# Where the product that sums the exponentials stands, and in which shape it runs, in a two-layer graph network kernel

## The chip, the cores and the metric

The kernel runs on one core of one Trainium2 chip. The metric is device time in microseconds of a whole execution, lower is better. A core has TensorE (PE, the matrix products; PEld are its weight loads), VectorE (DVE), ScalarE (ACT), GpSimd (POOL) and SyncE (SP, which here issues most of the transfers). Each engine works off its own queue of instructions in order, and waits on semaphores for others.

## The reference, cut to what matters

Sixteen graphs of 1024 nodes with 256 features go through an attention layer, whose queries come from a product with the weighted adjacency, and through a graph convolution with two batch norms. All is float32. The change lies in the softmax of the attention:

```
h  = relu(layernorm(x))                         # x: 16 x 1024 x 256
q  = relu((h^T @ (adj * A_s)) * para)           # 4 heads of 64
k, v = split(h @ kv_w)
attn = softmax(q @ k^T * scale, axis=-1)        # 1024 x 1024 for each head and graph
out  = attn @ v
x    = x + out
...                                             # layer 1: adjacency product, W1, batchnorm, W2, batchnorm
```

## The kernel before, in words

**Units and steps.** The attention works in units: one graph b, one chunk k of 128 features (two heads), and one half f of the queries (512 columns). There are 16 x 2 x 2 = 64 units. A unit takes four steps, each with two blocks of 128 keys. In a step, `scores` (line 882) makes the products sc of keys and queries, one for each head over 64 rows of the array, and ACT takes their exponentials p. One step later, `values` (line 922) multiplies them with v into o, one product for each head into 64 columns of the array. The scores are therefore laid out as keys by queries, and the softmax's denominators are sums over partitions and over key blocks.

**The denominators.** DVE adds the exponentials of all key blocks up in `acc` (`add`). When a unit has ended, `fold` (line 942) transposes `acc` in squares of 32 and adds along the rows, once for each head, into `part`: 128 partitions by 2 x 16 numbers. What is left is to add over groups of partitions. `sums` (line 953) does it with a product: the constant matrix `same` (line 82), 128 x 128, times `part`, 32 columns, into a PSUM tile of the pool `ps_t`. Three small DVE operations (lines 969, 974, 975) pick the right group and make the reciprocals `inv`. A step later, `finish` (line 980) turns the unit's output o with four transposes on PE (ot), into the same pool, which has one buffer, and `add_output` scales it by `inv` and adds it to x.

**Products in halves.** Nearly all other products of the first stage go through the helper `product` (line 167), which makes a product of 128 output rows as two matmuls of 64 columns of the array each. A float32 product appears in the trace as two records for each matmul.

**The order of the work.** The kernel's order is written by hand in `attention` (line 1008); nothing reorders it. In step s, PE gets in turn: the scores of step s; the actions filed under `at_top`; if the background has stopped at a mark `TOP`, its next piece, which is eight transposes htp of the next graph's features (`transposed`, line 385, called by `prepare` and `background`), copied out of PSUM by ACT; the values of step s - 1; and then pieces of the background (products pg, pk, pv, pa, py of the neighbouring graphs) until the step's share of their estimated time is used up. The actions of a unit whose values are issued in step s are filed by the tuple `one`: the two folds at the end of steps s and s + 1, the sums at the top of step s + 3, the output's transposes at the top of step s + 4. For the very last unit the four are at steps s, s, s + 1 and s + 1.

```
for action in at_top.pop(s, ()):
    action()
if top:
    done += advance(bg)
    top = False
if s in adds:
    adds.pop(s)()
```

Of the kernel before, what the change touches and what calls it, by code (L numbers as in the profile page):

```python
# [23 lines left out]
def gnn_two_layers_kernel(  # L24
# [12 lines left out]
    nc = tc.nc  # L37
# [37 lines left out]
    UNITS = B * CC * NH  # L75
# [20 lines left out]
    def layers(shifted):  # L96
# [35 lines left out]
        def advance(pieces):  # L132

            due = queue[:]
            queue.clear()
            cost = next(pieces, None)
            for action in due:
                action()
            return cost

        def run(*parts):
            for part in parts:
                while advance(part) is not None:
                    pass
            while queue:
                queue.pop(0)()
# [20 lines left out]
        def product(dst, left, right, start, stop):  # L167

            for e in range(2):
                r = slice(e * HW, (e + 1) * HW)  # L170
                nc.tensor.matmul(dst[r], left[:, r], right, start=start, stop=stop)  # L171
# [622 lines left out]
        def background(b):  # L794

            if b == 0:
                differences(1)
                for k in range(CC):
                    yield TOP
                    transposed(1, k)  # L800
                    yield 1.0
                w, products, norm = weighers[1], keys_values(1), Norm(2, True).all()
                yield from weave(
                    islice(products, 4), (0, double(islice(w, 8))), (0, islice(norm, 4))
                )
                yield from weave(
                    plain_queries(1), (0, norm), (0, w), (5, graph()), (7, degrees())
                )
                differences(2)
                yield from islice(products, 2)  # L810
                yield from prepare(2, products)
                return
            before = hidden(b - 1)
            gather = aggregate(b - 1)
            if b + 1 < B:
                w, products, norm = weighers[b + 1], keys_values(b + 1), normed(b - 1)
                yield from weave(islice(products, 4), (0, islice(w, 4)))
                if b == 1:
                    load_later()
                yield from weave(queries(b + 1), (0, double(w)), (9, islice(norm, 5)))  # L820
                yield next(gather)
                yield from weave(products, (0, norm))
            else:
                yield from weave(endings.pop(), (2, normed(b - 1)))
                yield next(gather)
            if b + 2 < B:
                yield from weave(gather, (3, summed(b + 2)))
                yield from prepare(b + 2, before)
            elif b + 2 == B:

                yield from gather
                endings.append(before)
            else:
                yield from gather
                yield from weave(before, (0, normed_last()))
# [46 lines left out]
        def scores(b, k, f, g):  # L882


            made = []
            for m in (2 * g, 2 * g + 1):
                sc = ps_sc.tile([P, 2, FB], F32, tag="sc", name=f"sc_{b}_{k}_{f}_{m}")
                for e in range(2):
                    r = slice(e * HD, (e + 1) * HD)
                    nc.tensor.matmul(  # L890
                        sc[:, e, :],
                        ks[b][k][r, m * P : (m + 1) * P],
                        qs[b][k][r, f * FB : (f + 1) * FB],
                        start=True,
                        stop=True,
                    )
                pr = p4.tile([P, 2, FB], F32, tag="p", name=f"p_{b}_{k}_{f}_{m}")
                nc.scalar.activation(pr, sc, AF.Exp)  # L898
                made.append(pr)
            return made  # L900

        class Unit:
# [50 lines left out]
            def sums(self):  # L953

                b, k, f = self.at
                J = FB // P
                if k == f == 0:
                    invs[b] = p2.tile([P, CC, NH, J, 2], F32, tag="inv", name=f"inv_{b}")
                self.inv = invs[b][:, k, f]
                pt = ps_t.tile([P, FB], F32, tag="t", name=f"sums_{self.name}")[:, : 2 * J * NS]  # L960
                nc.tensor.matmul(  # L961
                    pt,
                    same.rearrange("p a r -> p (a r)"),
                    self.part.rearrange("p e c -> p (e c)"),
                    start=True,
                    stop=True,
                )
                tmp = p1.tile([P, 2 * J, NS + 1], F32, tag="group", name=f"group_{self.name}")
                nc.vector.tensor_mul(
                    tmp[:, :, :NS],  # L970
                    pt.rearrange("p (c a) -> p c a", a=NS),
                    group.unsqueeze(1).to_broadcast([P, 2 * J, NS]),
                )
                nc.vector.tensor_reduce(tmp[:, :, NS], tmp[:, :, :NS], AX.X, ALU.add)
                nc.vector.reciprocal(
                    self.inv.rearrange("p j e -> p e j"),
                    tmp[:, :, NS].rearrange("p (e j) -> p e j", e=2),
                )
# [29 lines left out]
        def attention():  # L1008

            units = [Unit(b, k, f) for b in range(B) for k in range(CC) for f in range(NH)]  # L1010
            steps = [(u, g) for u in units for g in range(NG)]
            per_graph = CC * NH * NG
            before = None
            at_top, at_end, adds = {}, {}, {}
            bg, done, total, top = iter(()), 0.0, 0.0, False
            for s in range(len(steps) + 2):
                if s < len(steps):
                    unit, g = steps[s]
                    b = unit.at[0]
                    if s % per_graph == 0:  # L1020
                        run(bg)
                        top = False
                        bg, done = background(b), 0.0
                        total = (37.6 if b > 0 else 41.0) * (b + 1 < B) + 24.0 * (b > 0) + 6.0 * (b + 2 < B)
                        total += 13.7 * (0 < b < B - 2) + 27.4 * (b == B - 1) + 3.0 * (b == 0)

                        total -= 10.3 * (b == B - 1)
                    made = scores(*unit.at, g)
                    due = total * (s % per_graph + 1) / per_graph
                else:  # L1030
                    due += 5.1
                for action in at_top.pop(s, ()):
                    action()
                if top:
                    done += advance(bg)
                    top = False
                if s in adds:
                    adds.pop(s)()
                if s < len(steps):
                    for pr in made:  # L1040
                        unit.add(pr)
                if before is not None:
                    (last, g_last), prs = before
                    last.values(g_last, prs)
                    if g_last == NG - 1:

                        one = (0, 0, 1, 1) if last.index == UNITS - 1 else (0, 1, 3, 4)
                        for e in range(2):
                            at_end.setdefault(s + one[e], []).append(lambda u=last, e=e: u.fold(e))
                        at_top.setdefault(s + one[2], []).append(last.sums)  # L1050
                        at_top.setdefault(s + one[3], []).append(last.finish)
                        adds[s + one[3]] = last.add_output
                while done < due and not top:
                    cost = advance(bg)
                    if cost is None:
                        break
                    if cost == TOP:
                        top = True
                        break
                    done += cost  # L1060
                for action in at_end.pop(s, ()):
                    action()
                before = (steps[s], made) if s < len(steps) else None
            run(bg)
# [375 lines left out]
```

## Time and profile before

| what | value |
|---|---|
| time, median of 3 runs | 2608.92 us (2606.27 to 2610.16) |
| span of the profiled execution | 2604.3 us |
| granted TensorE clock, mean | 0.991 |
| score products (line 890) | 509.0 us busy, 2048 records |
| value products (line 931) | 495.9 us busy, 2048 records |
| sums (line 961) | 26.4 us busy, 128 records, mean 288 ns |
| weight loads of the sums (line 961) | 19.2 us busy, 128 records, mean 189 ns |
| output transposes ot (line 986) | 42.5 us busy, 256 records |
| feature transposes htp (line 396) | 36.5 us busy, 256 records |

The span runs from the first to the last instruction of the profiled execution; the runs' times hold a little more around it. Matmuls overlap, so a record's mean length is longer than its share of the busy time. A shape such as 128\*64 gives the rows and columns of the array that a matmul uses, and 128x32 behind it the data that streams through.

### The profile page before, as it was taken

The numbers are of one execution on the slowest core, as the hardware profiler recorded it, in microseconds if no ns is written. First come the engines' busy times: TensorE is split into PE (matmuls) and PEld (weight loads), VectorE is DVE, ScalarE is ACT, GpSimd is POOL, SyncE is SP. The second block draws the span as 40 slices with busy tenths as digits, with TensorE's granted clock in tenths as the row PEclk, the third lists the DMA queues.
The fourth block names the chain that finished last, engine by engine and source line by source line (L and its number), as shares of the span: only waits on it lengthen the run. The fifth ranks groups of instructions, "written<-read, shape, count | busy, mean of one in ns | idle before, by whom it ended". The sixth has DMA issues, their size and how long they took to land.

```text
span 2604.3 us, 31375 instructions
## 1 busy us (share of the span) xinstructions
PE 2525.9 (97%) x11627; PEld 931.8 (36%) x11627; DVE 1822.7 (70%) x2837; ACT 1460.7 (56%) x2034; POOL 391.3 (15%) x456
## 2 busy tenths in 40 slices
PE   7999999999999999999999999999999999999994
PEld 3333333333333333333333333333333333334443
DVE  4768686867767686868677676858686776657774
ACT  6774565647474746656464747465564634335543
POOL 1540001000101000010001010000100001036653
PEclk9999999999999999999999999999999999999997
DMA  3654224152524343241525243433315242355459
GB/s 138 229 171 173 93 99 154 54 189 73 182 83 152 111 148 101 102 150 55 183 71 182 86 156 107 147 100 114 137 62 180 66 166 105 109 196 221 170 198 367
DMA packets 130915, 363.46 MB, mean 140 GB/s; under 512 B 15288, under 2 KB 32192, under 8 KB 124608
## 3 DMA queue, kind: packets, MB, share of 16 engines
q1 hardware_dynamic: 110144, 282.70, 31.3%
q0 software_dynamic: 20608, 78.66, 7.9%
q8 instruction: 94, 1.54, 0.2%
q14 instruction: 69, 0.57, 0.1%
HBM read 286.79 MB, written 74.51 MB: 139 GB/s over the span
## 4 chain that ended last, share of the span: by engine, by line
PE 87%; ACT 7%; DMA 2%; issue 2%; DVE 1%; SPq 0%; POOL 0%; POOLq 0%; DVEq 0%; ACTq 0%
PE sc L890 17%; PE o L931 16%; PE pa L171 15%; PE pg L171 14%; PE py L171 8%; PE m_f L1235 7%; PE pk L171 4%; PE pv L171 4%; ACT w L458 3%; DMA out_dram<-xo_f 2%; ACT p L898 2%; PE ot L986 1%; ACT w L466 1%; PE sums L961 1%; ACT ht L399 1%
## 5 line engine op out<-in xcount | busy, mean ns | idle before, releaser
L898 ACT ACTIVATE p<-sc 128x1024 f32<-128x1024 f32 x512 | 495.0, 1020 | 452.5 <-PE sc L890 452.1
L920 DVE TENSOR_TENSOR acc<-acc,p 128x1024 f32<-128x1024 f32 x384 | 472.2, 1230 | 143.2 <-ACT p L898 121.8
L890 PE MATMUL sc<-q,k 64*128 64x512 f32 x2048 | 509.0, 615 | 4.7 <-ACT p L898 4.6
L931 PE MATMUL o<-p,v 128*64 128x512 f32 x2048 | 495.9, 605 | 0.0
L171 PE MATMUL pg<-w,h_a 128*64 128x512 f32 x1600 | 357.9, 592 | 3.1 <-DVE q L612 2.3
L171 PE MATMUL pa<-aht,h_b 128*64 128x512 f32 x1536 | 344.0, 592 | 3.5 <-ACT h_b L341 3.4
L890 PEld LDWEIGHTS sc<-q,k 64*128 64x128 f32 x2048 | 175.9, 186 | 325.5 <-issue 284.4
L458 ACT ACTIVATE w<-cbc,csum 128x512 f32<-128x512 f32 x256 | 285.5, 1168 | 0.0
L171 PE MATMUL py<-at,w 128*64 128x512 f32 x1024 | 232.8, 597 | 8.4 <-ACT ht L399 7.0
L445 DVE SCALAR_TENSOR_TENSOR w<-w,adj 128x1024 f32<-128x1024 f32 x128 | 157.5, 1230 | 114.8 <-ACT w L466 110.8
L931 PEld LDWEIGHTS o<-p,v 128*64 128x64 f32 x2048 | 124.1, 136 | 250.3 <-issue 247.2
L171 PEld LDWEIGHTS pg<-w,h_a 128*64 128x64 f32 x1600 | 114.7, 137 | 232.0 <-issue 214.4
L746 POOL DMA_DIRECT2D y_d<-y x128 | 70.5, 551 | 795.0 <-ACT y L745 787.2
L171 PEld LDWEIGHTS pa<-aht,h_b 128*64 128x64 f32 x1536 | 110.8, 137 | 216.9 <-issue 208.3
L745 ACT ACTIVATE y<-py,vec 128x512 f32<-128x512 f32 x128 | 87.6, 684 | 142.3 <-PE py L171 119.7
L749 DVE BATCH_NORM_STATS2 stats<-y 128x6 f32<-128x512 f32 x128 | 85.7, 687 | 79.6 <-ACT y L745 79.5
L466 ACT ACTIVATE w<-w 128x1024 f32<-128x1024 f32 x128 | 135.2, 1056 | 1.7
L520 DVE TENSOR_TENSOR w<-w,w 128x1024 f32<-128x1024 f32 x112 | 132.8, 1217 | 1.5
L341 ACT ACTIVATE h_b<-x,lnsm_b 128x256 f32<-128x256 f32 x128 | 70.4, 609 | 110.7 <-DVE lnsm_b L330 110.7
L93 POOL TENSOR_SCALAR lnsm_b<-mv_b 128x4 f32<-128x4 f32 x32 | 12.1, 379 | 791.5 <-DVE mv_b L319 791.4
L171 PEld LDWEIGHTS py<-at,w 128*64 128x64 f32 x1024 | 72.2, 137 | 162.4 <-issue 129.8
L171 PE MATMUL pk<-ht,kvw_f 128*64 128x512 f32 x512 | 117.0, 599 | 1.5 <-ACT ht L399 1.5
(158 smaller groups left out, 2779.7 us busy)
## 6 DMA issues: line engine op xcount, KB each, us to landing
aht<-aht_d SPq DMA_DIRECT2D x224, 512.0 KB, 6.3
adj<-in_adj_dram SPq DMA_DIRECT2D x128, 512.0 KB, 4.4
y_d<-y POOLq DMA_DIRECT2D x128, 256.0 KB, 2.6
yin_f<-y_d SPq DMA_DIRECT2D x32, 1024.0 KB, 6.3
x<-in_x_dram SPq DMA_DIRECT2D x32, 512.0 KB, 5.1
para<-in_para_dram SPq DMA_DIRECT2D x64, 256.0 KB, 3.9
x_d<-x POOLq DMA_DIRECT2D x16, 1024.0 KB, 10.3
xo_f<-x_d SPq DMA_DIRECT2D x32, 512.0 KB, 8.6
```

The costliest lines, as they stand in the source:

```text
L171: nc.tensor.matmul(dst[r], left[:, r], right, start=start, stop=stop)
L445: nc.vector.scalar_tensor_tensor(w, w, 1.0, a, op0=ALU.add, op1=ALU.mult)
L458: nc.scalar.activation(w[:, t, :].rearrange("p (t q) -> p t q", q=P), cbc[:, q * NT // NH : (q + 1) * NT // NH], AF.Abs, bias=csum[:, th * ...
L466: nc.scalar.activation(made[i], made[i], AF.Tanh, scale=-0.5 / C)
L520: nc.vector.tensor_sub(block(i)[part], block(x)[part], block(y)[part])
L745: nc.scalar.activation(y, made, AF.Identity, bias=b1[:, j : j + 1])
L749: nc.vector.bn_stats(stats1[:, j, i, :], y)
L890: nc.tensor.matmul(sc[:, e, :], ks[b][k][r, m * P : (m + 1) * P], qs[b][k][r, f * FB : (f + 1) * FB], start=True, stop=True,)
L898: nc.scalar.activation(pr, sc, AF.Exp)
L920: nc.vector.tensor_add(self.acc, self.acc, pr)
L931: nc.tensor.matmul(self.o[r, :], vs[b][k][:, m, r], pr[:, e, :], start=(m == 0), stop=(m == NT - 1),)
L1235: nc.tensor.matmul(made, left[:, j, :], right[:, j, :], start=(j == 0), stop=(j == JH - 1))
```

## The change

The product in `sums` goes through `product`: two matmuls of 64 columns each in place of one of 128, on the same operands and into the same PSUM tile. And the sums of all units but the last are filed in a new list, `at_mid`, which is worked off behind the piece of the background that `TOP` announces, and ahead of the addition of outputs, of the accumulation and of the values. In steps without such a piece the order of the instructions stays as it was. The sums of the last unit stay in `at_top`, and go through `product` as well.

```
@@ sums
-                nc.tensor.matmul(
+                product(
                     pt,
                     same.rearrange("p a r -> p (a r)"),
                     self.part.rearrange("p e c -> p (e c)"),
-                    start=True,
-                    stop=True,
+                    True,
+                    True,
                 )
@@ attention
-            at_top, at_end, adds = {}, {}, {}
+            at_top, at_mid, at_end, adds = {}, {}, {}, {}
...
                 if top:
                     done += advance(bg)
                     top = False
+                for action in at_mid.pop(s, ()):
+                    action()
                 if s in adds:
                     adds.pop(s)()
...
-                        at_top.setdefault(s + one[2], []).append(last.sums)
+                        (at_top if last.index == UNITS - 1 else at_mid).setdefault(
+                            s + one[2], []
+                        ).append(last.sums)
```

## The prediction

> **What bounds the kernel now.** I read the page's first part, then the chain that ended last, then the groups of TensorE (PE), then the timeline around the changed product.
>
> The page's busy times and its chain by engine and line:
>
> ```profile
> PE 2525.9 (97%) x11627; PEld 931.8 (36%) x11627; DVE 1822.7 (70%) x2837; ACT 1460.7 (56%) x2034; POOL 391.3 (15%) x456
> ...
> PE 87%; ACT 7%; DMA 2%; issue 2%; DVE 1%; SPq 0%; POOL 0%; POOLq 0%; DVEq 0%; ACTq 0%
> PE sc L890 17%; PE o L931 16%; PE pa L171 15%; PE pg L171 14%; PE py L171 8%; PE m_f L1235 7%; PE pk L171 4%; PE pv L171 4%; ACT w L458 3%; DMA out_dram<-xo_f 2%; ACT p L898 2%; PE ot L986 1%; ACT w L466 1%; PE sums L961 1%; ACT ht L399 1%
> ```
>
> PE is on 87% of the chain, and the sums have 1% of it. VectorE (DVE) and ScalarE (ACT) have room on average. So time taken from PE counts, except where another engine is ahead of it for a stretch.
>
> Now a step without sums, the PE timeline at 508 us and its weight loads (PEld); columns are start, length, instruction, count:
>
> ```profile
> 507.75 0.60 PE L890 MATMUL sc<-q,k 64*128 64x512 f32 x2
> 508.27 0.65 PE L931 MATMUL o<-p,v 128*64 128x512 f32 x2
> ...
> 508.27 0.20 PEld L931 LDWEIGHTS o<-p,v 128*64 128x64 f32 x4 [0.76 <-issue]
> ```
>
> and one with sums, at 526 us:
>
> ```profile
> 525.65 0.59 PE L890 MATMUL sc<-q,k 64*128 64x512 f32 x2
> 526.17 0.41 PE L961 MATMUL sums<-part,same 128*128 128x32 f32 x2
> 526.51 0.65 PE L931 MATMUL o<-p,v 128*64 128x512 f32 x2
> ...
> 526.17 0.30 PEld L961 LDWEIGHTS sums<-part,same 128*128 128x128 f32 x2 [0.76 <-issue]
> ```
>
> From the last score pair to the first value pair it is 0.52 us without sums and 0.86 us with them: the sums insert 0.34 us, though they stream only 32 columns, twice (each fp32 product appears as two records). The third field of the shape shows why: scores are 64*128, sums 128*128, values 128*64, three array shapes in a row.
>
> **The 0.34 us taken apart.** In a run of values, pairs start every 0.427 us for 512 columns (0.83 ns per column). So after a score pair starts, its streaming ends 0.43 us later, and the next shape's first weight load comes at 0.52: 0.09 us of drain at a change of shape. A 128-column load takes 0.11 us (two sums loads, mean 189 ns, span 0.30, so the second starts 0.11 after the first). A 64-column load takes about 0.055: the four of the values, mean 136, span 0.20, and record by record they come as two pairs, 0.055 apart, the halves of a pair 6 ns apart. So with full-width sums: load 0.108, load 0.110, stream 32 x 0.83 = 0.027, drain 0.093. Together 0.338, as measured.
>
> A step in which the background's transposes (htp) come after the sums, at 455 us:
>
> ```profile
> 455.02 0.41 PE L961 MATMUL sums<-part,same 128*128 128x32 f32 x2
> 455.26 1.07 PE L396 MATMUL htp<-ident,h_a 128*128 128x128 f32 x8
> 456.26 0.65 PE L931 MATMUL o<-p,v 128*64 128x512 f32 x2
> ```
>
> and the chain of waits across it:
>
> ```profile
> 452.09 2.33 ACT w L458 x2
> 454.42 0.58 ACT y L745
> 455.00 0.94 ACT w L466
> 455.94 0.47 ACT p L898
> 456.41 0.33 issue
> 456.74 1.03 ACT p L898
> 457.77 0.48 ACT ht L399
> 458.26 0.04 issue
> 458.30 1.93 PE py L171 x7
> ```
>
> Here ACT leads from 452.1 to 458.3, and PE's next product waits for its copy. The sums at 455.0 lie inside this stretch: what PE saves there is lost again.
>
> Following all 64 sums in the timeline: 49 are followed by values, 14 by htp, and the last by its own output transposes (ot). The insertion is 857 to 858 - 519 = 0.339 us in each of the 49, and 1763 (sums and htp) - 1543 (htp alone) = 0.220 us in the 14. All 14 lie in such ACT stretches, the first in a longer one from 160 to 174 us.
>
> **What the Trainium skill says.** "TensorEngine Tiling (Array Packing)", Key Properties: changing the tiling mode, not just the tile, drains the engine, and different tiles load weights and multiply in parallel. The trace agrees with both: 0.09 us of drain, and loads of two halves 6 ns apart. "TensorE: Matmul & The Clock Gate", LDWEIGHTS: load time is columns / 1.2 ns, so 107 and 53 ns; the trace shows 108 to 110 and 55. The same page, in Back-to-back issue gap, gives small matmuls a floor (25 ns start to start, or about 62 ns per MATMUL with one way of decoding); no row of this trace has four short matmuls in a row, so it is open here.
>
> **The change part by part.**
>
> 1. The split (63 sums, plus the last). Two full-width loads and two matmuls become four 64-column loads and four 32-column matmuls, in the shape of the values. The drain between sums and values goes; the one after the scores stays, as in a step without sums. With halves loading in parallel: after the drain, load pair one 0.055; load pair two 0.055, while pair one streams its 0.027; then the values' first load starts as pair two streams. Inserted: 0.110 us, since the values then need the same 0.055 of first load as without sums. Bounds: below, streaming and nothing else, 0.055; above, loads in series, 0.220; if a short matmul costs what a 128-column transpose costs with its load, 0.109 (the ot spacing), 4 x 0.109 = 0.436. I take 0.110, because values and all products of the helper show the halves loading together.
> Saved: 49 x (0.339 - 0.110) = 49 x 0.229 = 11.2 us.
>
> 2. The move behind the transposes (14 steps). The order there becomes scores, htp, sums, values. Nothing else is between the old and the new place on PE: no DMA is issued by the sums, and SP's and POOL's queues aren't passed. PE would save 0.220 - 0.110 = 0.11 us, but waits for ACT's copy anyway (from the start of the last value record to py's first at 458.30 it is 0.695 us, against 0.422 in steps where nothing is waited for, so 0.27 us is slack). I count 0, and up to 14 x 0.11 = 1.5 us if the stretch were shorter. The transposes come 0.22 us sooner; ACT reads them only behind its own queue, so this buys nothing.
> On DVE, the three small operations after the sums (186, 188, 204 ns) come about 1 us later in these steps, behind the transposes, and what stands behind them on DVE is the addition to acc. That one waits for the exponential p until 456.89 now; the three would end near 457.0. So 0.1 us late, on an engine with 30% idle time, read by no PE product within the step: 0.
>
> 3. Waits. The sums wait for the fold's part, made two steps earlier (18 us), so never in the 63; the last waits 5.0 us for DVE. In it the split gains or loses 0.1 us, once: 0. The output transposes come a whole step later than the sums and don't move. DVE now waits 65.4 us in all for the sums; PE sets that time and it doesn't matter to PE.
>
> What is late next: the same PE chain, with 0.23 us less per unit. The waits of PE in the trace (ACT's exponentials 4.6 us, ht 7.0, q 2.3 in all) each start from earlier PE work, so they move with it.
>
> Sum: 11.2 us. The profiled execution has a span of 2604.3; 2604.3 - 11.2 = 2593.1 expected. The runs' median is 2608.92, 4.6 above the span, and I carry that over: 2608.9 - 11.2 = 2597.7 us.
>
> **The rivals.**
>
> - Loads in series (0.220 inserted): 49 x 0.119 = 5.8, so 2603.1. For it: the loads of a half are long in the records (136 ns). Against: they start 6 ns apart, and a second pair follows at 0.055.
> - Cheaper still (0.055 inserted): 49 x 0.284 = 13.9, so 2595.0. For it: the weights of pair two and of the values could be loaded during the scores' drain. Against: the load of a new shape is never seen ahead of the drain.
> - The saving doesn't reach the end, because ACT or DVE set the pace all along as in the 14 steps: 2608.9. Against: the chain runs from PE to PE through the sums at 526.2 and elsewhere, and PE's listed waits add up to under 50 us of 2604.
> - Slower: the passes of the four short matmuls don't overlap. All write one bank and no long stream hides anything, so each would pay load, stream and drain, 0.055 + 0.027 + 0.093 = 0.175; four are 0.70. Then 49 x (0.70 - 0.339) = 17.7, and in the 13 ACT stretches of later graphs 0.48 - 0.27 slack = 0.21 each, 2.7: 2608.9 + 20.4 = 2629.3. It decides from an insertion of 0.339 us on. Against: full-width sums, also two passes into one bank, are explained without a drain between them, and pv's 256-column halves run back to back.
>
> **How the numbers follow.** Forecast 0.72 (its own range 2594 to 2601); loads in series 0.12; cheaper 0.05; no effect 0.04; slower 0.07. A measurement of this kernel can tell about 0.2% (5.2 us) from no change. Faster by more than that: 0.72 + 0.05 + half of the series case (2603.1 lies at the edge, 2603.7) = 0.83. Same: 0.06 + 0.04 = 0.10. Slower: 0.07. The runs before spread over 2606.3 to 2610.2, so I give each case about 2 us to both sides: 2592 to 2605 holds the first three cases, 0.89 less their tails.
>
> **What would show it.** In the changed profile the sums appear under the helper's line 171, as 128*64, x256, with 128x64 loads. From the last score pair to the first value pair it should be about 0.65 us in place of 0.86, and the first value pair shorter than 0.65 by some 0.03, because its load is partly covered. In the steps with htp the order is htp, sums, values, and py still waits for ht, a little longer. Sums at 0.70 us apiece, or a span near 2604, would make the prediction wrong; a gap of 0.76 means loads in series.

## The result, and the profile after

The changed kernel takes 2599.09 us (median of 5 runs, 2598.68 to 2600.80) against 2608.92 (5 runs, 2606.27 to 2610.16): ratio 0.9963, 95% interval 0.9951 to 0.9975. It is 9.8 us faster; 11.2 were forecast. The span of the profiled execution is 2597.2 us, 7.1 less than that of before.

The page of the changed kernel, busy times and the chain that ended last:

```profile
PE 2518.1 (97%) x11755; PEld 922.1 (36%) x11755; DVE 1822.0 (70%) x2837; ACT 1460.2 (56%) x2034; POOL 394.3 (15%) x456
...
PE sc L890 17%; PE o L931 16%; PE pa L171 15%; PE pg L171 14%; PE py L171 8%; PE m_f L1239 7%; PE pv L171 4%; PE pk L171 4%; ACT w L458 3%; DMA out_dram<-xo_f 2%; PE ot L986 1%; ACT p L898 1%; ACT w L466 1%; ACT ht L399 1%; PE sums L171 0%
```

PE has 128 records more and is busy 7.8 us less, and the sums have fallen from 1% of the chain to 0%. The timeline of PE and its weight loads in a step with sums and no transposes (start, length, instruction, count):

```profile
380.15 1.99 PE L890 MATMUL sc<-q,k 64*128 64x512 f32 x8
382.07 0.31 PE L171 MATMUL sums<-part,same 128*64 128x32 f32 x4
382.20 0.63 PE L931 MATMUL o<-p,v 128*64 128x512 f32 x2
...
382.07 0.20 PEld L171 LDWEIGHTS sums<-part,same 128*64 128x64 f32 x4 [0.76 <-issue]
382.18 0.20 PEld L931 LDWEIGHTS o<-p,v 128*64 128x64 f32 x4
```

From the start of the sums to that of the values it is now 0.13 us, where it was 0.34. The loads of the values start 0.11 us after those of the sums, without a drain between them. Record by record, the gap from the last score pair to the first value pair is 0.657 us in all 49 such steps (0.858 before), and the run of eight value records is 0.021 us shorter, since part of its first load is covered. So each of the 49 saves 0.201 + 0.021 = 0.222 us. (The gap is taken from the second record of the score pair; the two records of a pair start 6 to 7 ns apart.)

In the steps with transposes, the sums come behind them:

```profile
453.31 1.09 PE L396 MATMUL htp<-ident,h_a 128*128 128x128 f32 x8
454.33 0.31 PE L171 MATMUL sums<-part,same 128*64 128x32 f32 x4
454.47 1.92 PE L931 MATMUL o<-p,v 128*64 128x512 f32 x8
456.58 1.50 PE L171 MATMUL py<-at,w 128*64 128x512 f32 x5 [0.20 <-ACT ht L399]
```

PE gets to py sooner and waits there for ACT's copy ht: from the last value record to py 0.79 us, where it was 0.695.

**Where part of the gain went.** The starts of the score groups of both traces, step by step, give the lead of the changed kernel: how much sooner it gets to the same step. In graph 2 it is 1.23 us at the graph's start (before's 317.3 us), rises to 1.45 with the first sums (347), and falls back to 1.26 in the run of 48 pv records that comes next. The same run in the PE timelines of before and of after:

```profile
376.13 5.35 PE L171 MATMUL pv<-kvw_f,ht 128*64 128x256 f32 x48
381.41 1.99 PE L890 MATMUL sc<-q,k 64*128 64x512 f32 x8
```

```profile
374.68 5.54 PE L171 MATMUL pv<-kvw_f,ht 128*64 128x256 f32 x48
380.15 1.99 PE L890 MATMUL sc<-q,k 64*128 64x512 f32 x8
```

From start to next start it is 5.28 us before and 5.46 after, in each of 13 graphs (5.451 to 5.469). The time is lost at the 33rd record, the first into a PSUM bank that ACT must empty: 0.12 to 0.14 us of wait, and 0.051 because its weight load, which before began 0.06 to 0.08 us ahead of the record, now begins with it. ACT in the changed kernel just ahead of it, the product of DVE that ACT's q waits for, and DVE some steps earlier:

```profile
374.62 1.23 ACT L508 ACTIVATE q<-q 128x512 f32<-128x512 f32 x2 [0.36 <-DVE q L506]
375.76 1.92 ACT L898 ACTIVATE p<-sc 128x1024 f32<-128x1024 f32 x2
377.57 0.65 ACT L649 COPY v<-pv 128x256 f32<-128x256 f32 x2
...
373.93 1.26 DVE L506 TENSOR_TENSOR q<-q,para 128x512 f32<-128x512 f32 x2
...
356.79 0.68 DVE L539 TENSOR_TENSOR q<-pg,q 128x512 f32<-128x512 f32 x1
357.39 0.68 DVE L994 TENSOR_TENSOR os<-ot,inv 128x512 f32<-128x512 f32 x1
358.10 0.69 DVE L1000 TENSOR_TENSOR x<-os,x 128x512 f32<-128x512 f32 x1
358.71 0.18 DVE L1003 TENSOR_REDUCE seen<-inv 128x1 f32<-128x32 f32 x1
358.81 0.18 DVE L1004 TENSOR_REDUCE seen<-inv 128x1 f32<-128x32 f32 x1
```

The copy v that frees the bank ends at 378.22, behind the exponentials, behind q, which waits for DVE; where the 33rd record waits, it starts 0.05 us after this copy has ended. From 342.7 us to the q at 373.93, DVE is never idle for more than 0.11 us at a time. In the kernel before, the copy ended at 379.45 and the 33rd record came at 379.58, so the bank was free in time. The windows view of the kernel before, for the same stretch (length, then busy time and count of each engine, clock, share and rate of DMA), says it in one line:

```profile
342.60:378.30 35.70, 35.70 (x176) 12.61 (x174) 34.82 (x60) 14.67 (x18) 3.76 (x5) 1.00 0.06 20
```

DVE, the third engine of the line, is busy for 34.8 of 35.7 us: beside PE, it is the second engine at its bound here, though it has 30% of its time free over the whole. That it is DVE which takes the gain back is tested in experiments 3 to 5.

**The two spans.** A second place differs for another reason. The windows view shows the stretch behind PE's wait for the last norm (2.74 us idle, 3.3 us from record to record), first of before, then of after; the number behind POOL's is the granted clock:

```profile
2198.40:2201.80 3.40, 3.40 (x16) 1.13 (x16) 1.08 (x6) 2.18 (x5) 1.85 (x3) 1.00 0.16 46
```

```profile
2190.20:2193.60 3.40, 3.40 (x8) 0.61 (x8) 0.99 (x6) 2.18 (x5) 1.85 (x3) 0.50 0.09 36
```

The profiled execution of after ran 3.4 us there at half clock, and its eight pa records took 3.56 us in place of 1.87; that of before did not. This costs the span of after 1.7 us. It doesn't come from the new shapes: the experiment that only moves the sums had the same half clock at 2199.8 us with the old ones. What differs is where the wait falls. In all nine profiles the half clock begins a whole number of periods of 3.413 us after the clock's release at the start (in after 15.90 + 637 x 3.4133 = 2190.2 us), and what PE did in the period ahead of it goes with it. First the period of after, then two of before:

```profile
2186.77:2190.18 3.41, 0.67 (x6) 0.10 (x4) 3.27 (x10) 0.75 (x2) 0.00 (x0) 1.00 0.01 2
```

```profile
2194.04:2197.45 3.41, 1.58 (x8) 0.29 (x4) 3.31 (x7) 0.84 (x1) 0.75 (x1) 1.00 0.19 70
2197.45:2200.87 3.42, 2.50 (x12) 0.88 (x14) 1.89 (x9) 2.07 (x4) 1.54 (x3) 1.00 0.00 0
```

In after the wait fills one period, and PE is busy for 0.67 us of it; in before the border between two periods, counted from the release at 16.345, cuts the wait, and PE is busy for 1.58 and 2.50 us. So 7.1 + 1.7 = 8.8 us of the two spans stand for the change and the start. Of these, 0.24 us were there at the first score group, ahead of any sums, since the clock was released at 15.9 us in place of 16.3; 8.6 are left for the steps.

### The profile page after: what moved, and what is told of

Read it like the earlier page. It is cut to its first block, busy times and chain, and to the rows that moved or that the text cites. A ratio compares the mean times of both kernels' runs of the same rounds, so it can differ in the third digit from the quotient of the medians.

```text
span 2597.2 us, 31631 instructions
## 1 busy us (share of the span) xinstructions
PE 2518.1 (97%) x11755; PEld 922.1 (36%) x11755; DVE 1822.0 (70%) x2837; ACT 1460.2 (56%) x2034; POOL 394.3 (15%) x456
## 4 chain that ended last, share of the span: by engine, by line
PE 87%; ACT 7%; DMA 3%; issue 2%; DVE 1%; SPq 0%; POOL 0%; POOLq 0%; DVEq 0%; ACTq 0%
PE sc L890 17%; PE o L931 16%; PE pa L171 15%; PE pg L171 14%; PE py L171 8%; PE m_f L1239 7%; PE pv L171 4%; PE pk L171 4%; ACT w L458 3%; DMA out_dram<-xo_f 2%; PE ot L986 1%; ACT p L898 1%; ACT w L466 1%; ACT ht L399 1%; PE sums L171 0%
## 5 line engine op out<-in xcount | busy, mean ns | idle before, releaser
L171 PE MATMUL pv<-kvw_f,ht 128*64 128x256 f32 x1024 | 118.5, 380 | 0.0
```

## The experiments

**1. The split alone.** The sums go through the helper, but stay at the top of the step.

```
-                        (at_top if last.index == UNITS - 1 else at_mid).setdefault(
-                            s + one[2], []
-                        ).append(last.sums)
+                        at_top.setdefault(s + one[2], []).append(last.sums)
```

> The split without the move: the sums go through the helper in halves of 64 columns, but stay at the top of the step, ahead of the transposes. Theory (the gain is the shape change saved in the 49 steps without transposes; in the 14 others ACT sets the pace): the gap from the last score pair to the first value pair is 0.657 us in the 49 as in the changed kernel; in the 14 it is about 1.543 + 0.23 = 1.77 us, since the sums now stand between two changes of shape, and the wait of py for ht takes this up; the time is that of the changed kernel, 2599 us, within 1. Rival (the move carries part of it): about 14 x 0.11 = 1.5 us slower than the changed kernel or more, 2600.6 and up.

Measured: 2600.47 us (2599.19 to 2601.51), ratio 0.9966 (0.9952 to 0.9979). The gap is 0.657 us in the 49 steps and 1.782 in the 14, both as the theory said. The time isn't: it is 1.4 us above the changed kernel's, where 1 was allowed, and 0.1 below where the rival began; the runs of the two kernels overlap, so the times alone decide nothing. The profiles do. This one's span is 2.3 us longer. 1.46 us of that were there at the first score group: the clock was released at 18.8 us and not at 15.9, and half of the 2.9 us between is 1.47 (before the release, pairs of matmuls came every 0.85 us, after it every 0.43). Over steps 24 to 240 of the attention it falls 0.33 us behind. So the split is the gain, and the move is worth some 0.3 us in these two profiles.

**2. The move alone.** The sums stay one product of 128 columns, behind the transposes.

```
-                product(
+                nc.tensor.matmul(
...
-                    True,
-                    True,
+                    start=True,
+                    stop=True,
```

> The move without the split: the sums stay one product of 128 columns, but go behind the transposes. Theory: 0.858 us in the 49 steps as in the kernel before; in the 14 about 1.76 as before; the time is that of before, ratio 1.000. Rival (the move carries part of the gain): ratio 0.9994 or lower, with py waiting less for ht.

Measured: 2609.57 us (13 runs, 2606.44 to 2610.73), ratio 0.9999 (0.9991 to 1.0008). The gap in the 49 steps is 0.857; in the 14 it is 1.686, lower than I expected: the first weight load of the sums starts 0.11 us ahead of their first matmul, under the transposes, whose shape they have. Still nothing is gained, since py waits for ACT that much longer (0.77 us from the last value record, where it was 0.695): over steps 24 to 240 the profile is within 0.06 us of before's, and the time is that of before.

**3. Is it DVE that takes the gain back?** The two reductions into `seen`, which keep the largest and smallest reciprocal of a graph, are made half a graph later, where DVE has gaps.

```
-                if k == CC - 1 and f == NH - 1:
-                    inv = invs[b].rearrange("p k f j e -> p (k f j e)")
+                ready = [b - 1] if k == 0 and f == 1 and b > 0 else []
+                if b == B - 1 and k == CC - 1 and f == NH - 1:
+                    ready = [b]
+                for i in ready:
+                    inv = invs[i].rearrange("p k f j e -> p (k f j e)")
...
```

> The changed kernel, with the two small DVE reductions into the tile seen (0.18 us each, 0.19 us of the queue together), which stand at step 36 of each graph's end in a stretch where DVE is busy without a gap, made half a graph later where DVE has gaps. Nothing on PE is changed. Theory (once per graph, DVE is the bound for 35 us; PE's gain from the sums inside that stretch is lost in a run of 48 pv records, 5.46 us in place of 5.28, which waits for a PSUM bank that ACT empties late because ACT waited for DVE): DVE is 0.19 us earlier, the run of pv is back at 5.28 us, and 14 x 0.18 = 2.5 us are gained: 2596.6, ratio to before 0.9953. Rival (the 0.18 us come from PE's own queue or from the bank being used twice, whatever DVE does): the run of pv stays at 5.46 and the time at 2599.

Measured: 2597.18 us (2596.66 to 2597.41), ratio 0.9955 (0.9942 to 0.9969): 1.9 us below the changed kernel, and no run of the one reaches a run of the other. The PE timeline has the run of pv at its old length:

```profile
374.77 5.35 PE L171 MATMUL pv<-kvw_f,ht 128*64 128x256 f32 x48
380.06 1.99 PE L890 MATMUL sc<-q,k 64*128 64x512 f32 x8
```

5.28 us from start to start in all 13 graphs, and over steps 24 to 240 a lead of 2.1 us on the changed kernel. Not an instruction of PE was touched, so the rival, PE's own queue or the bank, falls.

**4. The same in the kernel before.** The edit is that of experiment 3.

> The same later place of the two DVE reductions, in the kernel before. Theory: before the change the bank came free 0.1 us ahead of PE, so PE did not wait in the pv run (5.28 us) and an earlier DVE buys nothing: ratio 1.000, pv 5.28. Rival (DVE's stretch bounds the graph in any case): 14 x 0.19 = 2.7 us faster, ratio 0.999.

Measured: 2609.51 us (13 runs, 2605.99 to 2610.56), ratio 1.0003 (0.9995 to 1.0012), pv 5.28 us. Before the change PE was late enough that the bank was free; the copy ended 0.11 to 0.13 us ahead of the 33rd record, and it needs 0.05, so the bound was hidden less than 0.1 us behind PE.

**5. More work for DVE at that place.** The changed kernel with the two reductions made three times.

```
+                    for _ in range(3):
-                    nc.vector.tensor_reduce(seen[:, 0, b : b + 1], inv, AX.X, ALU.max)
+                        nc.vector.tensor_reduce(seen[:, 0, b : b + 1], inv, AX.X, ALU.max)
...
```

> The changed kernel with the two small DVE reductions into seen made three times in place of once, in the same place: 4 more instructions on DVE for each graph, about 0.4 us of its queue. Theory (DVE bounds PE once per graph): the run of 48 pv records goes from 5.46 to about 5.85 us, 13 x 0.4 = 5 us slower than the changed kernel, 2604. Rival: pv stays at 5.46, 2599.

Measured: 2604.36 us (2603.87 to 2605.53), ratio 0.9983 (0.9976 to 0.9990). Now the wait is long enough to appear, in the timeline and in the list of PE's waits (us in total, times, longest):

```profile
375.19 3.62 PE L171 MATMUL pv<-kvw_f,ht 128*64 128x256 f32 x32
379.21 1.95 PE L171 MATMUL pv<-kvw_f,ht 128*64 128x256 f32 x16 [0.40 <-ACT v L649]
381.09 1.13 PE L890 MATMUL sc<-q,k 64*128 64x512 f32 x4
...
PE pv L171 <- ACT v L649: 5.3, 13, 0.4
```

The run takes 5.90 to 5.92 us, 0.45 more, for 0.42 us more of DVE's queue (four reductions, some 0.1 us apart), and the median is 5.3 us above the changed kernel's. What DVE is late there, PE is late.

**6. What a short pair costs.** The sums made twice in a row, over the same values.

```
+                for _ in range(2):
-                product(
+                    product(
...
```

> The changed kernel with the sums made twice in a row, the second time over the first with the same values: four short matmuls more in each of the 64 places. Theory (a pair of short matmuls costs the load of its 64 columns, 0.055 us, and the halves load together): the gap from the last score pair to the first value pair goes from 0.657 to 0.767 us, 49 x 0.11 = 5.4 us, less what DVE's stretch already takes (13 of them): about 4 us slower than the changed kernel, 2603. Rival 1 (halves load in series): 0.877, about 9 us slower. Rival 2 (a short pair costs only its streaming, 0.027): 0.711, about 2 us slower.

Measured: 2603.53 us (2602.74 to 2605.19), ratio 0.9983 (0.9975 to 0.9991), so 4.4 us over the changed kernel. The timeline has

```profile
380.44 1.99 PE L890 MATMUL sc<-q,k 64*128 64x512 f32 x8
382.36 0.42 PE L171 MATMUL sums<-part,same 128*64 128x32 f32 x8
382.61 0.63 PE L931 MATMUL o<-p,v 128*64 128x512 f32 x2
```

The gap is 0.773 us: two pairs more cost 0.116, so 0.058 a pair. That is the load of 64 columns; loads in series (0.877) and bare streaming (0.711) are both excluded. A pair is two matmuls, so one costs 29 ns, and the floor of about 62 ns that the prediction left open doesn't act here. In the steps with transposes the doubled sums add 0.12 us and py waits 0.11 us less, so there they cost next to nothing: ACT's lead takes up losses as it took up gains.

**7. A version that takes ACT out of the way.** Experiment 3, and DVE makes the copies ht from graph 2 on.

```
-                nc.scalar.copy(ht[:, g * FB : (g + 1) * FB], pt)
+                copy = nc.vector.tensor_copy if b >= 2 else nc.scalar.copy
+                copy(ht[:, g * FB : (g + 1) * FB], pt)
```

> The version with the later reductions, and besides the two copies of each transposed feature chunk (ht) made by DVE in place of ACT from graph 2 on. Theory (in the steps with transposes py waits for a PSUM bank that ACT's queue frees late, so PE's savings there are lost): from values to py it is 0.42 us in place of 1.13 and 0.79, PE gains up to 13 x (0.71 + 0.37) = 14 us, 2583 us, ratio 0.990. Rival (ACT is the bound of the whole stretch, whatever the copies do): PE waits for ACT a little later, at the scores or at the next py, and less than half of the 14 us is gained; or the copies make DVE late and PE waits for it.

Measured: 2587.59 us (2585.50 to 2588.54), ratio 0.9917 (0.9903 to 0.9930): 9.6 us below experiment 3, two thirds of what I expected. The second of the two waits of a graph is gone (0.79 to 0.42 us). The first went from 1.13 to 0.87 us only, which makes 13 x (0.37 + 0.26) = 8.2 us; over steps 24 to 240 the lead on experiment 3 is 8.5. The profile of experiment 3 has the half clock behind the last norm, and this one hasn't, which is worth 1.7 us of the span besides. PE now waits for DVE:

```profile
444.03 0.69 DVE L950 TENSOR_REDUCE part<-acc 128x16 f32<-128x512 f32 x1
444.64 1.28 DVE L400 COPY ht<-htp 128x512 f32<-128x512 f32 x2
445.37 1.94 PE L171 MATMUL py<-at,w 128*64 128x512 f32 x8 [0.28 <-DVE ht L400]
...
PE py L171 <- DVE ht L400: 3.6, 13, 0.3
```

The two copies start as soon as DVE has ended the fold, which stands ahead of them. The rival that ACT bounds the stretch whatever the copies do falls; the other, that the copies make DVE late and PE waits for it, is right for a part of the wait.

## Why the prediction was right, and where its size was off

**The split.** Right, and close: 0.117 us inserted (0.657 - 0.519 - 0.021) against the 0.110 of the sum, 0.222 saved against 0.229. The first value pair is 0.63 us long, 0.02 shorter, where some 0.03 was named. The Trainium skill, "TensorEngine Tiling (Array Packing)", Key Properties, was the right guide: the drain belongs to the change of shape. In the trace the loads of the values now follow those of the sums after 0.11 us, and experiment 2, which keeps the shape, keeps its full price in the 49 steps. Two things change at once, though, the shape and the width of the loads. Experiment 6 prices the two pairs at 0.116 us, where the prediction had 0.218 for two full loads; so by the prediction's terms about 0.10 of the 0.222 us is the cheaper loading and 0.12 the drain and the streaming that no longer stand in the open. This division is an estimate; no experiment changes one without the other.

**The 14 steps.** Right: nothing gained, and py waits longer by 0.10 us. Experiments 2 and 6 show it from both sides.

**The three DVE operations and the waits of the sums.** They cost nothing that the traces show. One reading was wrong: in the trace of before the fold's part is ready 2.6 to 8.6 us ahead of the 63 sums, half of them under 6.4, and not 18. It is early enough all the same.

**What failed.** The term 49 x 0.229 put all 49 sums on the path, with the remark that the same PE chain is late next and that DVE has room on average. In 13 graphs most of the saving of one of them is taken up by DVE's stretch: 13 x 0.18 = 2.3 us. The sum is then 49 x 0.222 - 2.3 = 10.9 - 2.3 = 8.6 us, and the spans give 8.6 for the steps. I had looked for the stretches where ACT leads by the waits that PE already had; a wait that would begin 0.1 us further on is in no list of waits. A windows view of each stage would have shown DVE at 98%.

**The time.** 2597.7 forecast, 2599.1 measured. I carried the 4.6 us between span and median over to the new kernel. That was wrong: in every execution on record with both numbers, the time stands 1.9 to 2.1 us above the span. The profiled execution of before was thus one of the shorter ones, about 2606.3. Of the 25 runs of before beside experiments 1 to 4, 7 lie at 2605.9 to 2606.6 and 18 at 2608.6 to 2610.6. What parts the two groups isn't shown for each run. The profile of experiment 2, an execution of 2610.65 us at the pace of before, gives one example: its span is 4.4 us longer than before's, 1.4 of it at the first score group after a later release of the clock, 1.7 at the half clock behind the last norm, and 1.3 behind the last scores. So the 9.8 us between the medians hold some 1.2 us that the change hasn't made by the account above, and that the measured gain lies nearer to the 11.2 forecast than the 8.6 of the steps do is luck. The error of the forecast was in the term of the 13 places; the medians hide half of it.

**The rivals.** Loads in series and cheaper loads are excluded by experiment 6. The slower case, each short matmul paying load, stream and drain, would have put the gap near 1.22 us; it is 0.657. "No effect" was true of the 14 steps, and of most of the saving of one more sum in each of 13 graphs (0.18 of 0.222 us).

## What to carry to other kernels

Where a small product stands between two products of other array shapes, try the shape of a neighbour. Here this took away one drain and half of the loading, though it made twice as many instructions: two short halves cost the load of one, 0.058 us. Before counting a saving on the busiest engine as many times as it occurs, look at each place for a second engine that has no gap there, and at how soon the buffers come free that PE will now ask for earlier. When the bound has moved to a second engine, taking even tiny operations out of its full stretch can pay: two of 0.18 us for each graph brought back 1.9 us here. And before two profiles are compared, look at their clocks from start to end.

## What the runs showed of the hardware

A 32-column pair of matmuls in halves costs 0.058 us, its weight load. Behind a wait of 3.3 us from record to record, the clock fell to half for 3.4 us in six of the nine profiles and not in the other three (before, experiments 4 and 7); in after, eight records then cost 1.7 us more. In the nine profiles, periods of 3.413 us counted from the release of the clock at the start tell the cases apart: from there to 2500 us, each stretch at half clock follows a period in which PE was busy for at most 1.43 us by the profile's modelled ends, and no period at full clock with 1.44 us or more was followed by one. In after, 0.67 us of PE in 2186.77 to 2190.18 were followed by half clock; in before, 1.58 and 2.50 us in two periods about the same wait were not. A PSUM wait of 0.12 to 0.14 us costs 0.17 to 0.19, since the next weight load can no longer hide.
